# Self-products kernel: flat output patterns for the tensor_tensors, and halves of a piece with equally many instructions

## The chip, the cores and the metric

The kernel runs on one NeuronCore of one Trainium2 chip. The metric is the device time of one execution in microseconds, the median of several runs. The profile is of one more execution with the hardware profiler on; its span is 1281.1 us, 2 us less than that median.

## The reference

For each of 4096 rows x of 256 float32 numbers the output holds all products x[i] * x[j] with i <= j, in the order of the upper triangle: row 0 of the triangle has 256 products, row 1 has 255, and so on, 32,896 numbers per row.

```python
def _L0_rec_ref(inputs):
    d = inputs.shape[1]
    dot = jnp.einsum('bi,bj->bij', inputs, inputs)
    iu, ju = jnp.triu_indices(d)
    return dot[:, iu, ju]
```

The input is 4.19 MB, the output 538.97 MB. Nothing but one multiplication is done per output number.

## The kernel before, in words

The 4096 rows are laid over the 128 partitions, 32 rows in each. The whole input is loaded once into the tile `x`, in three transfers (L122 to L125). Then 16 groups follow, and in each group every partition handles two of its rows (`REPEAT`). The 32,896 output columns are cut into five pieces of some 6,592 columns (`PIECES`, `even_borders`), so there are 80 pieces. A piece has an output tile `o` from a pool of three buffers (L129): 128 partitions x 2 rows x 6592 columns, 6592 KB. When it is full, one transfer issued by SyncE (L165) writes it out. Only the very first piece is cut into four transfers (`FIRST`), so that output starts early.

Inside a piece, `runs` gives the stretches of the triangle: for each i, the columns where x[i] is multiplied by x[j], x[j+1] and so on. These stretches are shared out:

- `split` gives the first few to ScalarE, as one ACTIVATE per stretch and row (L138).
- `vector_ops` gives the rest to VectorE in one of three forms. "each" is one tensor_scalar per row (L150). "all" is one tensor_tensor over both rows at once, with x[i] repeated by a step of 0 (L159). "two" is one tensor_tensor over both rows and over two neighbouring stretches at once, i and i+1; the second of the two is one number shorter, so that the write runs one number past it, and a later instruction overwrites that number.

`interleave` (L60 to L68) sets VectorE's order. It cuts the stretches of a piece into two halves, a and b, makes the instruction list of each, and deals them out in turn: a, b, a, b. In the version before, the cut is where half of the output columns lie on either side. Once one list is used up, the rest of the other follows by itself.

The framework (Tile) puts in all semaphore waits. Where it takes the output regions of two instructions on the same tile to overlap, the later one waits for the earlier, also if both run on VectorE. It also keeps the order of the loops within an engine only roughly: its scheduler lets VectorE begin the next piece's instructions between the last ones of a piece. The first ScalarE and the first VectorE instruction of a piece wait until the output transfer that used the buffer, three pieces before, has landed.

The change touches `interleave` and the output operand of the tensor_tensor (L159 to L164):

Of the kernel before, what the change touches and what calls it, by code (L numbers as in the profile page):

```python
# [1 line left out]

# [4 lines left out]

F32 = mybir.dt.float32
AF = mybir.ActivationFunctionType
ALU = mybir.AluOpType  # L10

P = 128
UNIT = 64
REPEAT = 2
PIECES = 5
BUDGET = 1.08
FIRST = [512, 1536, 3584]


def even_borders(lo: int, hi: int, pieces: int) -> list[int]:  # L20
    units = (hi - lo) // UNIT
    return [lo + units * c // pieces * UNIT for c in range(pieces)] + [hi]


def runs(d: int, lo: int, hi: int) -> list:


    found, at = [], 0
    for i in range(d):
        a, b = max(at, lo), min(at + d - i, hi)  # L30
        if a < b:
            found.append((i, i + a - at, a, b - a))
        at += d - i
    return found


def vector_ops(block: list) -> list:

    ops, k = [], 0
    while k < len(block):
        i, j, at, n = block[k]
        two = k + 2 < len(block) and i == j
        each = REPEAT * (130 + 0.52 * n)
        together = 68 + 1.046 * REPEAT * n - (34 if two else 0)
        if each <= together:
            ops.append(("each", block[k]))  # L50
        elif two:
            ops.append(("two", block[k]))
            k += 1
        else:
            ops.append(("all", block[k]))
        k += 1
    return ops


def interleave(block: list) -> list:  # L60


    half, at = 0, sum(n for *_, n in block) / 2
    while half < len(block) and at > 0:
        at -= block[half][3]
        half += 1
    a, b = vector_ops(block[:half]), vector_ops(block[half:])
    return [op for k in range(max(len(a), len(b))) for ops in (a, b) for op in ops[k : k + 1]]  # L68


def vector_time(block: list) -> float:
    t = 0.0
    for way, (i, j, at, n) in vector_ops(block):
        if way == "each":
            t += REPEAT * (130 + 0.52 * n)
        else:
            t += 68 + 1.046 * REPEAT * n * (2 if way == "two" else 1)
    return t


def split(block: list, budget: float) -> int:


    scalar, k = 0.0, 0
    while k < len(block):
        scalar += REPEAT * (184 + 0.837 * block[k][3])
        if vector_time(block[k:]) <= budget or scalar > vector_time(block[k + 1 :]):
            break
        k += 1
    return k  # L90


def window(ap: bass.AP, free: list) -> bass.AP:
    return bass.AP(ap.tensor, ap.offset, [list(ap.ap[0]), *free])


@with_exitstack
def kernel(
    ctx: ExitStack, tc: tile.TileContext, x: bass.AP, out: bass.AP
):  # L100

    nc = tc.nc
    n, d = x.shape
    width = out.shape[1]
    assert n % (P * REPEAT) == 0 and width == d * (d + 1) // 2 and width % UNIT == 0
    groups = n // (P * REPEAT)
    borders = even_borders(0, width, PIECES)  # L110
    slot = max(b - a for a, b in zip(borders, borders[1:]))

    xpool = ctx.enter_context(tc.tile_pool(name="x", bufs=1))
    opool = ctx.enter_context(tc.tile_pool(name="o", bufs=3))

    x_in = x.rearrange("(p r) d -> p (r d)", p=P)
    x_out = out.rearrange("(p g r) c -> g p r c", p=P, r=REPEAT)


    total = n // P * d  # L120
    xt = xpool.tile([P, total + 1], F32, name="x")
    nc.vector.memset(xt[:, total:], 0.0)  # L122
    cuts = [0, REPEAT * d, total // 2, total]
    for a, b in zip(cuts, cuts[1:]):
        nc.sync.dma_start(xt[:, a:b], x_in[:, a:b])  # L125

    for g in range(groups):
        for c, (lo, hi) in enumerate(zip(borders, borders[1:])):
            o = opool.tile([P, REPEAT, slot], F32, tag="o", name=f"o_{g}_{c}")  # L129
            first = g == c == 0  # L130
            cuts = [lo, *(FIRST if first else []), hi]
            for a, b in zip(cuts, cuts[1:]):
                block = runs(d, a, b)
                k = split(block, 0.0 if first else BUDGET * REPEAT * (b - a))
                for i, j, at, length in block[:k]:
                    for r in range(REPEAT):
                        row = (g * REPEAT + r) * d
                        nc.scalar.activation(  # L138
                            o[:, r, at - lo : at - lo + length],
                            xt[:, row + j : row + j + length],  # L140
                            AF.Copy,
                            scale=xt[:, row + i : row + i + 1],
                        )
                row = g * REPEAT * d
                for way, (i, j, at, length) in interleave(block[k:]):
                    at -= lo
                    if way == "each":
                        for r in range(REPEAT):
                            row_r = row + r * d
                            nc.vector.tensor_scalar(  # L150
                                o[:, r, at : at + length],
                                xt[:, row_r + j : row_r + j + length],
                                xt[:, row_r + i : row_r + i + 1],
                                None,
                                ALU.mult,
                            )
                        continue
                    m = 2 if way == "two" else 1
                    nc.vector.tensor_tensor(  # L159
                        o[:, :, at : at + m * length].rearrange("p r (m l) -> p r m l", m=m),  # L160
                        window(xt[:, row + j :], [[d, REPEAT], [1, m], [1, length]]),
                        window(xt[:, row + i :], [[d, REPEAT], [1, m], [0, length]]),
                        ALU.mult,
                    )  # L164
                nc.sync.dma_start(x_out[g][:, :, a:b], o[:, :, a - lo : b - lo])  # L165


# [1 line left out]
_INS = ["r_inputs"]  # L169
_OUTS = [((4096, 32896), "float32")]  # L170


# [20 lines left out]
```

## Time and profile before

| what | before |
|---|---|
| time, median of 3 | 1283.14 us (1283.05 to 1283.23) |
| span of the profile | 1281.1 us |
| VectorE busy | 1218.6 us, 2962 instructions |
| ScalarE busy | 234.7 us, 787 instructions |
| output transfers of 6592 KB | 64, median 23.3 us from issue to landing |
| bytes moved | 543.43 MB, mean 424 GB/s |

In the profile DVE is VectorE, ACT is ScalarE, SPq the queue of transfers that SyncE issues. "L159 DVE ... o<-x" is a group of instructions of line 159 that write `o` from `x`. The chain is followed back from the last instruction, at each step to what released it; "issue" in it is time in which the engine waited for nothing that the profile shows. A wait for something on the engine itself can appear there.

In the trace, an instruction's start and duration overlap those of the next where the two are pipelined, so the start-to-start distance tells more than the duration.

### The profile page before, as it was taken

How to read it: one execution, taken by the hardware profiler on the slowest of the kernel's cores; microseconds unless marked ns; L12 is line 12 of the kernel's file. 1: busy time of each engine (PE TensorE's matmuls, PEld its weight loads, DVE VectorE, ACT ScalarE, POOL GpSimd, SP SyncE). 2: the span in 40 equal slices, each digit the busy share in tenths (PEclk: the TensorE clock that was granted, in tenths of full speed). 3: DMA queues.
4: the chain of work that ended last, by engine and by line, in shares of the span. 5: the costliest groups of instructions: out<-in, count | busy, mean ns of one | idle time of the engine just before them, and what ended most of it. 6: DMA issues, size and time to landing. Idle time of an engine off the chain costs nothing.

```text
span 1281.1 us, 4091 instructions
## 1 busy us (share of the span) xinstructions
DVE 1218.6 (95%) x2962; ACT 234.7 (18%) x787; POOL 0.2 (0%) x4
## 2 busy tenths in 40 slices
DVE  8999999999999999999999999999999999999993
ACT  4201213012121211212012130121301213012130
POOL 0000000000000000000000000000000000000000
DMA  9999999999999999999999999999999999999999
GB/s 384 404 395 433 422 432 435 421 432 423 431 423 422 433 422 432 435 418 425 433 430 426 425 429 422 433 434 421 422 428 426 435 420 434 423 433 422 432 423 395
DMA packets 23040, 543.43 MB, mean 424 GB/s; under 512 B 1376, under 2 KB 1376, under 8 KB 2016
## 3 DMA queue, kind: packets, MB, share of 16 engines
q1 hardware_dynamic: 23008, 543.17, 99.2%
q14 instruction: 32, 0.26, 0.1%
HBM read 4.19 MB, written 538.97 MB: 424 GB/s over the span
## 4 chain that ended last, share of the span: by engine, by line
DVE 95%; issue 3%; DVEq 0%
DVE o L159 69%; DVE o L150 26%; DVEq L159 0%
## 5 line engine op out<-in xcount | busy, mean ns | idle before, releaser
L159 DVE TENSOR_TENSOR o<-x 128x2 f32<-128x2 f32 (+51 forms) x1635 | 908.6, 568 | 37.7 <-DVE o L159 0.5
L138 ACT ACTIVATE o<-x 128x197 f32<-128x197 f32 (+25 forms) x786 | 233.4, 384 | 1005.5 <-DMA out_dram<-o 790.9
L150 DVE TENSOR_SCALAR o<-x 128x216 f32<-128x216 f32 (+6 forms) x1326 | 360.8, 331 | 3.5 <-DMA x<-in_r_inputs_dram 2.5
L138 ACT ACT_TABLE_LOAD x1 | 1.3, 1283 | 0.7 <-PEq L180 0.7
L122 DVE MEMSET x<- 128x1 f32 x1 | 0.1, 59 | 0.8 <-PEq L180 0.8
L180 POOL MEMSET const-bfloat16-1.0<- 128x1 bf16 x1 | 0.1, 101 | 0.0
L180 POOL MEMSET const-uint8-127<- 128x1 uint8 x1 | 0.1, 101 | 0.0
L180 POOL MEMSET const-float32-0.0<- 128x1 f32 x1 | 0.1, 98 | 0.2 <-issue 0.2
L180 POOL MEMSET const-float32-1.0<- 128x1 f32 x1 | 0.1, 98 | 0.0
## 6 DMA issues: line engine op xcount, KB each, us to landing
out_dram<-o SPq DMA_DIRECT2D x64, 6592.0 KB, 23.3
out_dram<-o SPq DMA_DIRECT2D x15, 6528.0 KB, 23.3
out_dram<-o SPq DMA_DIRECT2D x1, 2944.0 KB, 17.3
x<-in_r_inputs_dram SPq DMA_DIRECT2D x1, 2048.0 KB, 12.7
out_dram<-o SPq DMA_DIRECT2D x1, 2048.0 KB, 14.3
x<-in_r_inputs_dram SPq DMA_DIRECT2D x1, 1792.0 KB, 7.1
out_dram<-o SPq DMA_DIRECT2D x1, 1024.0 KB, 11.9
out_dram<-o SPq DMA_DIRECT2D x1, 512.0 KB, 11.1
```

Of the source, the lines that this page charges most:

```text
L122: nc.vector.memset(xt[:, total:], 0.0)
L138: nc.scalar.activation(o[:, r, at - lo : at - lo + length], xt[:, row + j : row + j + length], AF.Copy, scale=xt[:, row + i : row + i + 1],)
L150: nc.vector.tensor_scalar(o[:, r, at : at + length], xt[:, row_r + j : row_r + j + length], xt[:, row_r + i : row_r + i + 1], None, ALU.mult,)
L159: nc.vector.tensor_tensor(o[:, :, at : at + m * length].rearrange("p r (m l) -> p r m l", m=m), window(xt[:, row + j :], [[d, REPEAT], [1, ...
L180: nc = _bacc.Bacc("TRN2", target_bir_lowering=False, num_devices=1)
```

## The change

Two edits. The first gives the tensor_tensor its output as a flat pattern, partition x row x column. Before, the columns were split in the pattern into m stretches of one length (m is 1 or 2), as in the input patterns; the numbers written and their addresses are the same. The second cuts a piece where the two halves have about equally many VectorE instructions, instead of equally many columns: it moves the cut down from the end of the piece until the first list is no longer than the second. Both are meant to make instructions that follow each other on VectorE independent, so that none has to wait for the one in front of it.

```diff
 def interleave(block: list) -> list:
-    half, at = 0, sum(n for *_, n in block) / 2
-    while half < len(block) and at > 0:
-        at -= block[half][3]
-        half += 1
+    half = len(block)
+    while half and len(vector_ops(block[:half])) > len(vector_ops(block[half:])):
+        half -= 1
     a, b = vector_ops(block[:half]), vector_ops(block[half:])
     return [op for k in range(max(len(a), len(b))) for ops in (a, b) for op in ops[k : k + 1]]
...
                     nc.vector.tensor_tensor(
-                        o[:, :, at : at + m * length].rearrange("p r (m l) -> p r m l", m=m),
+                        o[:, :, at : at + m * length],
                         window(xt[:, row + j :], [[d, REPEAT], [1, m], [1, length]]),
                         window(xt[:, row + i :], [[d, REPEAT], [1, m], [0, length]]),
                         ALU.mult,
                     )
```

## The prediction

> **What bounds the kernel now.** I read the page first (busy shares, slices, queues, chain), then the waits, then the chain piece by piece, then stretches of the DMA.
>
> ```profile
> DVE 1218.6 (95%) x2962; ACT 234.7 (18%) x787; POOL 0.2 (0%) x4
> ...
> q1 hardware_dynamic: 23008, 543.17, 99.2%
> ...
> DVE 95%; issue 3%; DVEq 0%
> DVE o L159 69%; DVE o L150 26%; DVEq L159 0%
> ...
> L159 DVE TENSOR_TENSOR o<-x 128x2 f32<-128x2 f32 (+51 forms) x1635 | 908.6, 568 | 37.7 <-DVE o L159 0.5
> L138 ACT ACTIVATE o<-x 128x197 f32<-128x197 f32 (+25 forms) x786 | 233.4, 384 | 1005.5 <-DMA out_dram<-o 790.9
> ```
>
> Two resources are nearly full at once: VectorE 95%, the output queue 99.2%. The chain is VectorE alone from start to end. Which of the two the other follows is told by who waits:
>
> ```profile
> ACT o L138 <- DMA out_dram<-o: 790.9, 47, 24.8
> ...
> DVE o L150 <- DMA x<-in_r_inputs_dram: 2.5, 1, 2.5
> ```
> ```profile
> SPq L165 <- DVE o L159: 844.6, 51, 20.5
> SPq L165 <- DVE o L150: 378.2, 32, 14.2
> ```
>
> VectorE never waits for a landed output (its only DMA wait is the first load), while the output queue waits for VectorE before nearly every issue. So VectorE sets the pace, and the DMA engines follow with little to spare. Issue to landing is 23.3 us for a transfer that itself takes 15.6 to 15.7 us, so usually one is in flight and the next is queued.
>
> The chain in order of time shows what VectorE loses (start, length, what):
>
> ```profile
> 36.71 0.94 DVE o L159
> 37.66 0.02 issue
> 37.68 0.88 DVE o L159
> 38.56 0.02 issue
> ...
> 39.42 6.83 DVE o L159 x11
> 46.25 0.02 issue
> 46.27 0.72 DVE o L159
> 47.00 0.02 issue
> 47.02 0.80 DVE o L159
> ```
>
> Up to 38.6 each tensor_tensor begins only after its predecessor has ended, with a sliver of "issue" between. From 39.42, where two pieces happen to be interleaved, eleven run as one unbroken stretch: each starts about 82 ns BEFORE the end of the one ahead. From 46.27 they are held again. The built program says why: the held ones wait on VectorE's own semaphore for the instruction just in front of them; those of the unbroken stretch wait for the one two back or for none.
>
> Where the DMA has holes (stretch, length, VectorE, ACT, POOL, clock, DMA share, GB/s):
>
> ```profile
> 13.00:40.00 27.00, 26.52 (x52) 2.95 (x9) 0.00 (x0) 1.00 1.01 430
> 40.00:48.00 8.00, 7.90 (x14) 2.03 (x8) 0.00 (x0) 1.00 0.79 336
> 48.00:80.00 32.00, 30.69 (x84) 7.23 (x27) 0.00 (x0) 1.00 0.93 396
> 80.00:1181.00 1101.00, 1066.97 (x2590) 197.36 (x669) 0.00 (x0) 1.00 1.00 427
> ```
>
> Full, the queue moves 430 GB/s (13 to 40 us; the share passes 1 because packets overlap slightly at the hand-over). It ran dry near 45 and 79 us; afterwards it loses only a little.
>
> **What the Trainium skill says.** "Vector Engine (DVE) Microarchitecture Reference", 5.2 Measured stream behaviour on trn2, puts one- and two-source operations at 1.0417 ns per column plus about 75 ns each when queued. The trace agrees: unheld tensor_tensors step by 1.042 ns per element plus 69 to 76 ns. "Perfetto Trace Analysis", DVE / Act Engine Instruction: the reported end is the write acknowledgement, the next instruction may prefetch before it, and a semaphore is pushed only at it. That fits both gaps: -82 ns unheld, +34 ns held. "VectorE: DVE Perf Modes", The DRAIN you can't avoid, says chaining without semaphores saves nothing; this trace disagrees by about 0.12 us per held pair, and the measurement decides. "SBUF — State Buffer", Who interferes with whom: DMA does not contend with a compute engine. The trace has 26,368-byte packets at a median 982 ns whether the VectorE instruction running is held, unheld or a tensor_scalar.
>
> **The change part by part.**
>
> *Waits removed.* In the program before, 1041 tensor_tensors and 30 tensor_scalars wait for the instruction directly in front. In the changed program none does; its waits on VectorE reach two or three back. Start to start, with 1.042 ns per element taken off, a held pair costs 193 ns and an unheld one 69; same-size pairs agree (a 632-element tensor_tensor is followed after 0.73 us at 39.42, where the next is unheld, and after 0.85 us at 120.56, where it is held). So 1071 x 0.12 = 129 us, by the 0.124 us of the medians 133 us. I take 131.
>
> *Waits two back.* Such tensor_tensors step by the same 69 ns in the trace of before: free. Where the intervening one has under about 40 elements a stall of up to 46 ns is possible; some six per group of rows, 16 groups: under 5 us of VectorE, hidden by the slack below.
>
> *Instructions added.* 16 tensor_tensors (1651 for 1635) since the new halves pair rows differently: 16 x 0.07 = 1 us. The split between ScalarE and VectorE, element counts, transfers and load order stay.
>
> *Sum on VectorE.* Its stream is 1257 us long now (3.3 to 1260.6); after, 1257 - 131 + 1 = about 1127, or 14.1 us per piece over 80 pieces. By piece of a group: 13.8, 14.2, 14.1, 14.1, 14.2, where today it is 13.8, 14.6, 16.1, 16.8, 17.5.
>
> *What takes over.* The transfer of a piece costs 15.6 to 15.7 us, so VectorE is now 1.5 us faster per piece than the queue, and all but the DMA's own holes is absorbed. With three buffers VectorE builds up a lead until it has to wait for the landing of the output three back. That wait is new. Behind it stand all later VectorE work and ScalarE's share (at most 9 us, in parallel), and the queue waits for both; but when a buffer comes free one transfer has just begun and another is finished and queued. Refilling takes 14 us, due after 31. So it stands 15 us off the path: cost nothing.
>
> *What the end gains: the holes.* From the packet records I added up, microsecond by microsecond, the DMA engines without a packet (sixteenths of the sixteen): 2.1 us before the first load arrives, 1.8 at 40 to 60 us, 2.5 at 60 to 90, 6.1 at 90 to 1180 (nearly all at the end of a group of five pieces, 0.3 to 0.8 us each time, where the fifth piece comes 21 us after the fourth), 0.5 at 1180 to 1260, 1.0 at the end. Start and end stay. The rest, 10.9 us, goes if each piece is issued over 1.2 us before the first engine finishes the one ahead, which is what the trace needs for no hole. Tightest is the third piece, issued at 45.6 now. It sheds 12 held waits (1.5 us) and, by the changed program's order, four tensor_tensors of the fourth piece that run ahead of its end (2.7 us), so it is issued at 41.4, against a first engine done at 44.8. It holds, and later pieces have more room. 1283.1 - 10.9 = 1272.2.
>
> *Second way.* Mean landing to mean landing without a hole takes 15.70 us (6592 KB) or 15.54 (6528 KB). After the second piece's mean landing at 45.15 come 63 and 15 of them: 45.15 + 989.1 + 233.1 = 1267.4; the slowest engine lands 0.9 later, the span ends 1.0 after that, and the time is 2.0 over the span: 1271.3. I take **1272**.
>
> **The rivals.**
> *A, the queue gains only part.* The slowest engine is about 1 us behind the median at most landings and catches up in the holes; instruction-fetch packets delay single engines. Without holes the lag may grow. Packets during unheld tensor_tensors average 988 ns, during held ones 984: 0.4% of 1265 us is 5 us. Either gives 1276 to 1277. Against it: the difference is in the restart after a hole, and the median is the same.
> *B, no gain.* If the queue's 99.2% were its true limit and the missing 0.8% came back elsewhere, 1283. For it: that share. Against: the 40 to 48 us stretch at 0.79, and holes that coincide with late issues.
> *C, slower.* The new wait puts landing, refill and issue in series. Were one buffer in effect always held by ScalarE's in-order work, two would rotate: (14.1 + 15.7 + 2.0) / 2 = 15.9 us per piece, 0.2 x 80 = 16 us over the forecast, 1288. Against: ScalarE does one piece in 3 to 9 us.
>
> **How the numbers follow.** Forecast 0.80, A 0.09, B 0.05, C 0.04, and 0.02 that it falls below the two sums. The low end, 1269.8, is the second sum less the 1 to 2 us that engine lag and start-up leave open; the high end, 1277, is A's. Faster 0.91 (forecast, A, below), same 0.05, slower 0.04.
>
> **What would show it.** VectorE busy near 1127 us (89%), with no "issue" pieces between tensor_tensors; new rows of VectorE waiting for landed outputs, some 105 us in all (VectorE done at about 1236, less 3 at the start, less 1127); issue to landing up from 23 to about 32 us (one queued piece more); 40 to 80 us full, GB/s near 430 throughout; the last issue some 33 us before the last landing instead of 19. Wrong if the slices dip again at group ends, if packets lengthen past 982 ns, or if VectorE stays near 1200.

## The result, and the profile after

The changed kernel takes 1277.89 us (four runs, 1277.80 to 1277.92) against 1283.16 us for the kernel before on the same chip: a ratio of 0.9959, 95% interval 0.9942 to 0.9976. It is 5.3 us faster. The forecast was 1272, with a range of 1269.8 to 1277.0: the direction was right, the gain about half of the 11 us that were forecast, and the time lies 0.9 us above the range.

The page of the changed kernel, the lines that answer to those shown of the kernel before (lines moved up by one, so L158 is the tensor_tensor and L149 the tensor_scalar):

```profile
span 1276.1 us, 4106 instructions
...
DVE 1128.9 (88%) x2978; ACT 234.7 (18%) x787; POOL 0.2 (0%) x4
...
GB/s 385 433 434 430 428 432 426 433 426 433 428 430 432 427 434 423 435 426 432 428 430 431 427 435 424 434 425 434 429 430 432 426 433 424 434 428 432 430 428 314
...
q1 hardware_dynamic: 23008, 543.17, 99.5%
q14 instruction: 32, 0.26, 0.0%
...
DMA 62%; DVE 35%; issue 0%; DVEq 0%; SPq 0%
...
out_dram<-o SPq DMA_DIRECT2D x64, 6592.0 KB, 33.0
```

VectorE is busy for 90 us less. The chain that ended last is now mostly DMA, with no "issue" share. From issue to landing a transfer takes 33.0 us for 23.3, since more is queued ahead of it. And the last of the forty slices falls to 314 GB/s. In the kernel before it was 395. That slice turns out to hold the missing gain.

The waits of the changed kernel (in us, times, longest) show the new wait that the prediction expected:

```profile
DVE o L158 <- DMA out_dram<-o: 59.3, 42, 2.1
DVE o L149 <- DMA out_dram<-o: 50.4, 28, 2.5
```

VectorE waits for landed outputs, 110 us in all. The chain from 27 to 62 us no longer has a sliver of "issue" between one tensor_tensor and the next:

```profile
27.13 13.56 DVE o L158 x18
...
40.95 13.55 DVE o L158 x23
```

Eighteen tensor_tensors run as one stretch, where the kernel before had a gap ahead of nearly each.

The DMA by stretches (stretch, length, VectorE, ACT, POOL, clock, DMA share, GB/s), the same four as before and two at the end:

```profile
13.00:40.00 27.00, 27.00 (x56) 3.25 (x10) 0.00 (x0) 1.00 1.02 432
40.00:48.00 8.00, 8.00 (x14) 2.19 (x9) 0.00 (x0) 1.00 0.99 428
48.00:80.00 32.00, 32.00 (x107) 7.34 (x27) 0.00 (x0) 1.00 1.00 432
80.00:1181.00 1101.00, 995.38 (x2633) 197.08 (x668) 0.00 (x0) 1.00 1.00 430
1256.00:1267.00 11.00, 0.00 (x0) 0.00 (x0) 0.00 (x0) 1.00 0.98 422
1269.00:1275.00 6.00, 0.00 (x0) 0.00 (x0) 0.00 (x0) 1.00 0.05 22
```

The 6 us ahead of the last landing of the kernel before, for comparison:

```profile
1273.00:1279.00 6.00, 0.00 (x0) 0.00 (x0) 0.00 (x0) 1.00 0.84 360
```

The holes at 45 and 79 us are gone and the queue runs at 430 GB/s throughout. Between 40 and 1260 us, the time that DMA engines spend without a packet has fallen from 10 to 11 us (the prediction's count was 10.9) to under 1 us. But for the last 6 us the DMA share is 0.05, close to one sixteenth: a single DMA engine is still working while fifteen are done. Of the last transfer's sixteen completions the median lands at 1267.6, the fifteenth at 1269.7 and the last at 1275.2. In the kernel before the three were 1279.0, 1279.4 and 1280.1.

### The profile page after: what moved, and what is told of

Read it like the earlier page. It is cut to its first block, busy times and chain, and to the rows that moved or that the text cites. A ratio compares the mean times of both kernels' runs of the same rounds, so it can differ in the third digit from the quotient of the medians.

```text
span 1276.1 us, 4106 instructions
## 1 busy us (share of the span) xinstructions
DVE 1128.9 (88%) x2978; ACT 234.7 (18%) x787; POOL 0.2 (0%) x4
## 4 chain that ended last, share of the span: by engine, by line
DMA 62%; DVE 35%; issue 0%; DVEq 0%; SPq 0%
DMA out_dram<-o 62%; DVE o L158 24%; DVE o L149 11%; DMA x<-in_r_inputs_dram 0%; SPq L164 0%; DVEq L158 0%; DVEq L149 0%; DVEq L188 0%
## 5 line engine op out<-in xcount | busy, mean ns | idle before, releaser
L158 DVE TENSOR_TENSOR o<-x 128x104 f32<-128x104 f32 (+60 forms) x1651 | 804.2, 559 | 59.3 <-DMA out_dram<-o 59.3
L149 DVE TENSOR_SCALAR o<-x 128x216 f32<-128x216 f32 (+5 forms) x1326 | 344.9, 333 | 53.1 <-DMA out_dram<-o 50.4
```

What stands on the lines that cost most here:

```text
L149: nc.vector.tensor_scalar(o[:, r, at : at + length], xt[:, row_r + j : row_r + j + length], xt[:, row_r + i : row_r + i + 1], None, ALU.mult,)
L158: nc.vector.tensor_tensor(o[:, :, at : at + m * length], window(xt[:, row + j :], [[d, REPEAT], [1, m], [1, length]]), window(xt[:, row + ...
```

## The experiments

The landing records tell how that engine fell behind. They hold sixteen completions for each transfer, without the engine's number. I follow the latest one and call its engine A. Its lag over the median is 0.7 us at the second piece (45 us), 2.3 at 249 us, 4.1 at 566, 5.7 at 880, 7.5 at 1197 and 7.6 at the end. It does not lose steadily. From one 6592 KB transfer to the next it takes 15.55 us (15.40 for 6528 KB), less than the 15.70 of the median, except for 23 transfers that take it some 0.8 us more. In each of those, or within the landing's own latency before it, the records show a packet of the instruction queue (q14): 8 KB, 309 ns. Such a packet is called a block below. An output packet then starts exactly at its end and mostly lasts about 1335 ns for the usual 982. By the Trainium skill ("Perfetto Trace Analysis", The 4-stage abstract model) an instruction has 64 bytes, so 8 KB are 128 of them; VectorE has 3049 here with its waits, 23 whole blocks: as many as the steps.

The packet records tell the same from another side. They have no engine's number either, but on one engine a packet begins within some 5 ns of the end of the one ahead, so the packets can be strung together. After 630 us 12 blocks come each time that VectorE has begun some 128 more instructions. Eleven of them lie on the string that ends last; the twelfth can't be placed. The last three that fall due by ScalarE's count lie on the string that ends second to last, 2.1 us behind. The two kinds differ in the output packet that follows: it lasts 1328 ns or more behind VectorE's 23 blocks, and 1081 to 1165 behind ScalarE's 7.

Theory F: each block of VectorE's instructions is fetched by the same DMA engine and sets it back 0.8 us. In the kernel before, the queue's holes let it catch up; with a full queue nothing does. Rival S: one engine is slower by nature when it never rests. Rival C (another one than C of the prediction): VectorE's dense traffic slows the DMA. Five groups of runs separate these and take the change apart. They were made on several chips, on which the kernel before took 1282.9 to 1283.4 us, so between groups a difference of half a microsecond means nothing.

**Transfers alone, and transfers with instructions.** Four kernels leave out all products and keep the transfers. They differ in the number of tiny memsets.

```diff
+                if done < 3:
+                    (nc.gpsimd if done == 1 else nc.vector).memset(o[:, :, a - lo : slot if b == hi else b - lo], 1.0)
+                else:
+                    nc.vector.memset(o[:, :, 0:1], 1.0)
                 nc.sync.dma_start(x_out[g][:, :, a:b], o[:, :, a - lo : b - lo])
```

> This kernel leaves out all products: three tiles are filled with ones, and the same 86 transfers are issued, with one tiny memset per piece so that each still waits for the landing three pieces before. VectorE has 168 instructions instead of 3049. Theory F (each 8 KB block of VectorE instructions fetched, one per 128 instructions, sets back one DMA engine by about 0.8 us, and a queue without holes never lets it catch up): slowest engine within 1.5 us of the median at the last landing, 1271 to 1273 us. Rival S (one DMA engine is simply slower when it never rests, whatever VectorE does): lag 6 to 8 us, 1278. Rival C (VectorE's dense traffic on SBUF slows the queue): as F in time, but the packets shorter than the changed kernel's 982 ns median.

Measured: 1269.83 us, engine A 0.5 us behind at the last landing. Packets have a median of 981 ns against 982. So S falls: with a queue that never rests and hardly any instructions, no engine falls behind. From 1267.2 us on the queue is empty, and no engine works on alone (the line is without the ACT column, which had no work):

```profile
1267.00:1268.00 1.00, 0.00 (x0) 0.00 (x0) 1.00 0.00 0
```

It ended 1.2 us below F's window. The landing of the median, 1266.6, is 1.0 us earlier than in the changed kernel.

```diff
+            for k in range(36):
+                nc.vector.memset(spare[:, 16 * k : 16 * k + 1], 1.0)
```

> As the run without products, which it leaves out too, plus 36 one-column memsets per piece on a spare tile, so that VectorE has 3037 instructions but next to no data traffic. F: 23 blocks fetched, slowest engine 6 to 7 us behind, 1277 to 1279 us. S: the same as without them. C: the same as without them, 1271 to 1273.

Measured: 1285.57 us, slower than any theory said. The memsets wrote a tile of their own, so nothing held them back and VectorE ran them all in the first 190 us. 23 blocks came within that time, from 37 us on one every 5.5 to 9.5 us. By then one engine was 17.6 us behind and another 9.6. Both stayed about there: 16.2 and 7.9 us at the end. For engine A the 0.8 us per block hold here too: between 30 and 188 us 22 blocks came and its lag grew by 16.9 us, with ten transfers in which it could regain 0.15. What F had wrong in this run is the regaining. It counted on 78 transfers of it, but engine A regained 1.9 us up to 514 us and then no more, so that 16 us were left instead of 6 or 7. The second engine took no part in the blocks: strung together, the 18 blocks between 30 and 150 us all lie on engine A, while the second was already 7 us behind. Its packets are longer where many memsets run: those in which 32 or more of them begin average 1087 ns (51 packets), and on another engine 978. Why they are is open. For even spacing the memsets had to go into the piece's own tile (36 of them, 72 in a second run):

```diff
+                for k in range(36 if done > 2 else 0):
+                    nc.vector.memset(o[:, 0:1, 64 * k + 64 : 64 * k + 65], 1.0)
                 nc.sync.dma_start(x_out[g][:, :, a:b], o[:, :, a - lo : b - lo])
```

> No products, as in the run of transfers alone, plus 36 one-column memsets per piece written into the piece's own tile, so that they are spread over the whole run and not run ahead. 3037 VectorE instructions, as many as the changed kernel, no data traffic to speak of. F: slowest engine 6 to 8 us behind the median, 1276 to 1279 us. If the changed kernel's lag came from VectorE's or ScalarE's data traffic: 1270.

Measured: 1277.07 us, engine A 7.7 us behind. VectorE is busy for 105.5 us in all, and ScalarE does nothing. At the end one engine works alone again (the last line, with the DMA share at 0.06):

```profile
DVE 105.5 (8%) x2855; POOL 11.3 (1%) x5
...
q14 instruction: 24, 0.20, 0.0%
...
1268.00:1274.00 6.00, 0.00 (x0) 0.00 (x0) 1.00 0.06 26
```

A kernel that computes nothing, with as many VectorE instructions as the changed one, has the changed kernel's lag to 0.1 us. By the packet that follows, 23 of its blocks are of VectorE's kind and none of ScalarE's. C falls.

> The same with 72 memsets per piece, 5800 VectorE instructions, 45 blocks. F, with each block adding 0.8 us and 0.15 us regained per piece, as the changed kernel's landings have it: 45 x 0.8 - 78 x 0.15 = 24 us behind, 1294 us. If the loss per block is the 0.3 us of the block's own packet: 14 us behind, 1283. If the lag doesn't grow with the blocks: as with 36.

Measured: 1294.05 us, engine A 24.7 us behind; F said 24 us and 1294. Its page has 46 packets in the instruction queue for 24, and the two stretches at its end show engine A alone for 12 us (lines as above, without the ACT column, which had no work):

```profile
q14 instruction: 46, 0.38, 0.1%
```
```profile
1256.00:1266.00 10.00, 0.00 (x0) 0.00 (x0) 1.00 0.99 425
1268.00:1276.00 8.00, 0.00 (x0) 0.00 (x0) 1.00 0.12 53
1279.00:1291.00 12.00, 0.00 (x0) 0.00 (x0) 1.00 0.06 26
```

From 1268 to 1276 two engines run (0.12), then one (0.06). The time rose with the number of blocks by the predicted steps, so "0.8 us per block, 0.15 us regained per transfer" held in both runs with memsets spread evenly.

**More instructions beside the real work.**

```diff
+                for k in range(18 if g else 0):
+                    nc.vector.memset(spare[:, 16 * k : 16 * k + 1], 1.0)
                 nc.sync.dma_start(x_out[g][:, :, a:b], o[:, :, a - lo : b - lo])
```

> The changed kernel plus 18 one-column memsets per piece from the second group on, 1350 VectorE instructions more (about 1.3 us per piece, within VectorE's slack of 1.5). F: 10.5 blocks more, 8.4 us more lag on the one engine, 1285 to 1287 us. S and C: no change, 1278 (up to 1279 if VectorE's lead gets thin).

Measured: 1286.61 us, the number that F expected, but not for F's reason. Engine A ended 7.6 us behind, as in the changed kernel. The median itself landed 8.5 us later, since VectorE, with 1.3 us more per piece and the memsets ahead of their time, ran short between 150 and 280 us, and the queue with it:

```profile
13.00:80.00 67.00, 66.84 (x291) 12.09 (x43) 0.00 (x0) 1.00 1.01 432
80.00:330.00 250.00, 249.77 (x1780) 43.02 (x146) 0.00 (x0) 1.00 0.97 415
330.00:1268.00 938.00, 833.40 (x2180) 168.76 (x572) 0.00 (x0) 1.00 1.00 430
```

VectorE is busy for all 250 us of the second stretch, which is where the DMA share falls. In those holes engine A caught up. The final time says nothing for or against F. The way there speaks for it: at 178 us, before the worst of the holes, engine A was already 7.1 us behind, where the changed kernel had 2.3 at 172 us.

**Fewer instructions on VectorE.**

```diff
-BUDGET = 1.08
+BUDGET = 0.75
```

> The changed kernel with BUDGET 0.75 for 1.08: VectorE 2296 instructions for 3049, ScalarE 2299 for 859, VectorE 829 us of work for 1123. F with ScalarE's blocks fetched through another DMA engine: VectorE's engine sheds 4.6 us, ScalarE's gains some, 1273 to 1275 us. F with all blocks through the same engine: 6 blocks more, about 1283. S: 1278. C: 1272 to 1274, but with shorter packets.

Measured: 1274.72 us, ratio to the kernel before 0.9936 (0.9922 to 0.9951). Two engines ended 5.2 and 4.9 us behind, a third 3.4, the rest 0.3 or less. With 18 blocks each on VectorE and ScalarE, two late engines fit one for each instruction stream, and the packets bear this out. Behind 17 blocks the next output packet is of VectorE's kind (1328 ns or more), behind 17 of ScalarE's (1081 to 1119). All 12 of VectorE's kind that can be placed on a late engine lie on the string that ends last, and none of ScalarE's does; ScalarE's seven after 727 us lie on the string that ends second to last. The third engine is not explained.

```diff
-        each = REPEAT * (130 + 0.52 * n)
-        together = 68 + 1.046 * REPEAT * n - (34 if two else 0)
-        if each <= together:
-            ops.append(("each", block[k]))
-        elif two:
+        if two:
```

> The changed kernel without the form that takes one tensor_scalar per row: VectorE uses tensor_tensors for all its stretches. Its stream stays 1122 us by the trace's steps, its instructions fall from 3049 to 2090. F: 7.5 blocks fewer at 0.8 us: the slowest engine lands 6.0 us sooner, 1271.9 us. If blocks don't matter with real work running: 1278.

Measured: 1275.34 us, ratio 0.9937 (0.9923 to 0.9952). The direction is F's, the size is not: 2.5 us gained instead of 6.0. Engine A ended 4.6 us behind. Its steps say where the rest went: there are 15 of them instead of 23, as counted, but a step is now 1.0 us (16.42 for the 15.40 of a 6528 KB transfer), not 0.8. The packets show where it is lost: ahead of 13 of 16 blocks of VectorE's kind one more output packet is long, 1120 to 1200 ns for 982, as ahead of none of the changed kernel's 23. Why it is isn't known.

```diff
+                for q in range(13 if g else 0):
+                    nc.vector.memset(o[:, 0:1, b - lo - 64 * q - 1 : b - lo - 64 * q], 1.0)
                 row = g * REPEAT * d
```

> The same plus 13 one-column memsets per piece from the second group on, overwritten by later products, which brings VectorE back to 3065 instructions and adds 0.9 us per piece, within its slack. F: the gain is gone, 1277.5 to 1278.5 us. If the gain came from the tensor_tensors' pattern or from fewer waits: as without the memsets.

Measured: 1278.23 us, engine A 7.3 us behind. 975 memsets of one column each, in VectorE's slack, took the gain back and the lag with it. The gain of the run before lies in the number of instructions, not in their form.

> Tensor_tensors throughout and BUDGET 1.00 for 1.08: VectorE 1994 instructions, ScalarE 1349 for 937. F: 0.7 of a block less on VectorE's engine, 3 more on ScalarE's, which has room: 1271 to 1272.5 us; the floor is the 1269.8 of the transfers alone.

Measured: 1275.03 us, engine A 4.7 us behind, 2.5 us above the expected window for the same reason as the run with BUDGET 1.08: the 15 blocks of VectorE cost more than 0.8 us each. Ahead of 11 of them stands such a long packet.

> Tensor_tensors throughout and BUDGET 0.90: VectorE 1852 instructions, ScalarE 1855, so 14.5 blocks each and on different DMA engines. F with 0.8 to 1.0 us per block: both engines 3 to 4 us behind the median at the end, 1273 to 1274.5 us, below the 1274.7 of BUDGET 0.75 with 18 blocks each. If ScalarE's blocks go through VectorE's engine: 1279 or more.

Measured: 1273.21 us (1273.10 to 1273.34), ratio to the kernel before 0.9922 (0.9909 to 0.9936). The two slowest engines are 3.7 and 3.6 us behind. It is the fastest kernel of the study that computes the products, 4.7 us under the changed kernel and some 3 above the transfers alone.

```profile
DVE 946.3 (74%) x1766; ACT 564.4 (44%) x1767; POOL 0.2 (0%) x4
```

The steps of engine A (transfers that take it over 0.5 us more than its usual 15.55 or 15.40), counted in the landings of eight kernels:

| kernel | VectorE instructions / 128 | steps | mean step, us | lag at the end, us | time, us |
|---|---|---|---|---|---|
| changed kernel | 23.8 | 23 | 0.81 | 7.6 | 1277.89 |
| transfers, 36 memsets | 23.7 | 23 | 0.80 | 7.7 | 1277.07 |
| transfers, 72 memsets | 45.3 | 44 | 0.79 | 24.7 | 1294.05 |
| tensor_tensors with 13 memsets | 23.9 | 23 | 0.81 | 7.3 | 1278.23 |
| BUDGET 0.75 | 17.9 | 17 | 0.88 | 5.2 | 1274.72 |
| tensor_tensors | 16.3 | 15 | 1.00 | 4.6 | 1275.34 |
| tensor_tensors, BUDGET 1.00 | 15.6 | 15 | 0.99 | 4.7 | 1275.03 |
| tensor_tensors, BUDGET 0.90 | 14.5 | 13 | 0.89 | 3.7 | 1273.21 |

The number of steps follows the number of blocks in every row, and each step has a block's packet with it. The size of a step is 0.8 where blocks are many and up to 1.0 where they are fewer.

**Each edit of the change alone.**

```diff
-                        o[:, :, at : at + m * length].rearrange("p r (m l) -> p r m l", m=m),
+                        o[:, :, at : at + m * length],
```

> The first edit alone: flat output patterns, cut at half the columns. By the built program 304 held waits are left of 1071, VectorE's stream 1159 us, 14.6 us per piece, still ahead of the queue's 15.7. If the queue's slowest engine sets the end and VectorE no longer matters (F): as the changed kernel, 1277.5 to 1279 us. If VectorE's remaining held waits (fifth piece 16.5 us) still open holes: 1279 to 1281.

Measured: 1277.75 us, ratio 0.9957 (0.9943 to 0.9972), engine A 7.65 us behind: the changed kernel's time to 0.14 us. VectorE is busy for 1153.9 us, 25 us more than with both edits, and none of it shows.

```diff
-    half, at = 0, sum(n for *_, n in block) / 2
-    while half < len(block) and at > 0:
-        at -= block[half][3]
-        half += 1
+    half = len(block)
+    while half and len(vector_ops(block[:half])) > len(vector_ops(block[half:])):
+        half -= 1
```

> The second edit alone: halves with equally many instructions, output still in the split pattern. By the built program 930 held waits of 1071 are left, VectorE's stream 1241 us, 15.5 us per piece, just under the queue's 15.7. F: VectorE's lead is thin, so the first holes stay and later ones shrink: 1278 to 1281 us. If the edit did nothing alone: 1283.

Measured: 1279.88 us, ratio 0.9974 (0.9963 to 0.9984). Its 2.0 us over the changed kernel are one hole:

```profile
13.00:28.00 15.00, 15.00 (x38) 0.68 (x2) 0.00 (x0) 1.00 1.00 420
28.00:32.00 4.00, 3.93 (x9) 1.70 (x6) 0.00 (x0) 1.00 0.48 206
32.00:80.00 48.00, 46.49 (x107) 9.87 (x36) 0.00 (x0) 1.00 1.01 430
```

The second piece is issued at 30.2 instead of 27.5 us and the queue is half empty from 28 to 32. After that it is as full as with both edits, and engine A ends 6.8 us behind.

## Why the prediction was right or wrong

**Right: the held waits and their price.** Of VectorE's busy time 1128.9 us is left; the sum said 1127. Neighbouring tensor_tensors of the changed kernel step by a median of 68.6 ns plus the elements (68 to 70 for four in five pairs), as the unheld ones did before, at 69. (One reading was off by a hair: at 120.56 us the next begins after 0.84 us, not 0.85.)

**Right: what takes over.** VectorE waits 110 us for landings (105 expected), issue to landing is 33.0 us (32), the last issue comes 33.0 us before the last landing (33). The new wait costs nothing: the queue is never short. Rival C of the prediction, a slower kernel by a rotation of two buffers, did not occur.

**Right: the holes.** The third piece is issued at 41.6 us (41.4). Nearly all of the 10.9 us of holes are gone: the median landing of the last transfer comes 11.4 us sooner. The mean landing of the last transfer came at 1268.3 us, where the second way said 1267.4.

**Wrong: "the slowest engine lands 0.9 later".** That term of the second way measured 6.9 us, and the same fault is in "The rest, 10.9 us, goes". Both treat the sixteen engines as one. The time is set by the slowest, and engine A had far less to gain than the mean. Its own sum from the second piece's landing at 45.7, by its steps: 63 x 15.55 + 15 x 15.40 + 23 x 0.8 = 1229.1, so 1274.8 without any hole; measured 1275.2. In the kernel before its last landing was 1280.1, so the gain there was 4.9 us, 5.3 on the time.

Where were those 4.9 us? Nearly all in the ramp. Transfer by transfer, the latest completion of the changed kernel comes 0.2 us sooner than before at 46 us, 3.5 at 97 and 4.1 at 145. In the remaining 1135 us it gains only 0.9 more, while the median goes on from 4.9 to 11.4. In steady state engine A was already full: a group of five takes it 4 x 15.55 + 15.40 = 77.6 us plus 1.5 blocks at 0.8, that is 78.8 us by the steps of the changed kernel, and VectorE's period before was 78.83 us. What looked like holes of the queue at the ends of groups were holes of the other fifteen: engine A did not catch up in them, as theory F has it, the others waited there.

**Rival A named the mechanism but did not size it.** It said that instruction-fetch packets delay single engines and the lag may grow without holes, and gave 1276 to 1277 on a chance of 0.09. The only working that it shows for the figure is packets 0.4% longer, and these did not come: 6592 KB transfers have packets of 984.7 ns on average after the change, 985.0 before. That it lies near the result is luck. With 23 blocks at 0.8 us the mechanism gives 1277.8, the 1274.8 of engine A's sum and the prediction's 1.0 and 2.0 on top. The 0.8 is of the changed kernel, though. The kernel before shows the steps (some of its latest completions take 16.5 us where the usual step is 15.55), but mixed with the holes: its 23 average 0.94, too much by 3 us in the sum.

## What to carry to other kernels

A queue that is full on average can have one engine that was full already; before taking holes as gain, follow the latest of the sixteen completions, not their mean. Once transfers bind, the number of instructions is itself a cost on the DMA side, even of those that hide behind a transfer: fewer and longer instructions, or a spread over two engines, gained 4.7 us over the changed kernel here, where 25 us more or less of VectorE time (the first edit alone) moved nothing.

## What the runs showed of the hardware that was not expected

- A block of 8 KB of VectorE instructions costs one DMA engine 0.8 to 1.0 us of a full queue, although its own packet takes 309 ns; the output packet behind it takes some 350 ns longer than usual. That held with blocks 6 to 10 us apart as with blocks 54 us apart. Where it is 1.0, a packet ahead of the block is longer too. ScalarE's blocks go through another engine, and the packet behind them is some 110 ns longer.
- Between blocks the engine that is behind takes 15.55 us per transfer and the others 15.70. In the run where all blocks came early, engine A was later at 15.69 and stayed 16 us behind. What decides this is open.
- In the run with 72 memsets per piece a second engine lost 0.13 us in each transfer, with or without a block. Its packets in which 32 or more memsets begin average 1095 ns (63 packets), those in which fewer than four begin 980; on another engine both kinds stay at 981 to 984. Why the memsets lengthen the packets of that one engine is open.
- The Trainium skill's "DMA: Bandwidth & Descriptors", Where 436 GB/s comes from, puts the ports' ceiling at 435 GB/s. The full queue measured 430 here, over 1101 us.
